# Twelve-layer decoder on one core: where keys, gathered sums, constants and scalings stand in the order of the work

## The chip, the cores and the metric

The kernel runs on one core of a Trainium2 chip, in one launch. The metric is the device time of that core in microseconds (us); the time of a kernel is the median of its runs. TensorE (PE in the profile, PEld for its weight loads), VectorE (DVE), ScalarE (ACT), GpSimd (POOL) and SyncE (SP) each work through their own queue in order, and wait for one another by semaphores.

## The reference

A stack of four decoder layers L0 to L3 on x of shape 8 x 256 x 256 (batches, tokens, features), with a context of 8 x 77 x 256. Each layer has three parts, and every part ends in the same step:

```
x = _layernorm(x + attn(x))
x = _layernorm(x + xattn(x, ctx))
x = _layernorm(x + ffn(x))
```

The parts differ by layer. What matters here:

- L0's and L1's cross-attention have 16 heads of 64 on the context, L1's with a mask. L0's FFN is a mixture of 8 experts, top 2, with GELU; L1's has 8 experts with a capacity and a shared part.
- L1's self-attention is causal softmax attention with 16 heads of 16. L2's self-attention is linear attention with exponential features: keys' features times values are summed first, and the queries' features are multiplied with the sums.
- L2's FFN has 14 routed experts, top 2, and two shared ones that all tokens pass; each is `silu(rms(x) * rw @ W1) @ W2`.
- L3's attention is a state-space block: an RMS norm with weight, an input projection, a short convolution, and decayed sums over chunks of 64 tokens. L3's cross-attention takes the softmax of q within heads and of k over the context, multiplies q with the sums of k and v, and adds q to the result ahead of the output projection.

In an expert layer a token's two results are fetched and added with their weights: `x += w0 * y0 + w1 * y1`, then the norm.

## The kernel before

The 2048 tokens are 16 tiles of 128 tokens (`X[i]`, tokens on the partitions) and four blocks of 512 (`XT`, features on the partitions). `NB` is the eight batches, two tiles each. One class, `Build`, holds the whole kernel; each layer is a method, called in order from `build` (L2705 to 2740). Weights come from a pool `wp` of five buffers of 128 x 2048 (`load_w`, issued on SP). PSUM is a pool of eight banks (`ps`). `mm` at L156 issues the matmuls of most products, `transpose_to` (L294) and `put_xT` (L236) the transposes; their copies out of PSUM alternate between VectorE (L142) and ScalarE (L144). A norm is VectorE's statistics (L250, L252), a power on GpSimd (`rs`, L183 and L184), and VectorE's scaling (L256).

The order of work is written with generators. `later(gen)` puts a generator in a list, `tick` advances the first, `wave` all of them, and `settle` runs them out. A scheduler then orders the instructions on each engine, so neighbours in the source may end apart. `self.mark` names an instruction after which others may be held, with `after`.

**The gathered sums.** `collected` (L2676) gives them batch by batch: for each of two tiles and each of two results an indirect gather on GpSimd (`gy`, L1057), an add on VectorE (L2686), then the norm. `collect(route, behind)` starts it with the first batch. `need(b)` transposes batch b (`put_xT`) and begins the sums of batch b + 1. If `gate` is set, the next add waits for it, and each add becomes the gate of the next one. `gates` holds single ones.

**L0's FFN** (L1136). It computes the keys of L1's cross-attention from the context (`context_keys`, L828: eight slices in two halves of two accumulating matmul pairs each, copied with a bias by ScalarE at L1147), then runs the routed tiles of 256 tokens (`some_tiles`, L1099). For each tile `fetch` gathers an expert's W1, W2 and biases `more` (L1039), and `fetch_x` its tokens (`gx`, L1057); `turned` transposes them; `each(j)` does what goes between tiles. `biased` (L1155, L1157) adds the output biases of the experts after the tiles.

**L1's self-attention** (L1217). Ahead of its loop stand the constants: `mxp` and `vp` set to zeros and ones by GpSimd (L1230, L1233, L1234), masks `later` and `unit` by VectorE. For each batch `project_in` makes k, q, v (L1257, L1262, L1267), `shift` takes the row maxima of the scores (L1287, maxima at L1291) and puts them into the queries (L1300), `weights` the exponentials, `weigh` the result. The loop runs `weights(b)`, then `project_in` and `shift` of b + 1, then `weigh(b)`. `gate` is set to the maxima of batch 0 once, ahead of the loop.

**Routing** (`Routing.batch`). Scores, top 2, the chosen experts' indicators `rsel` (L2541), then a product with a triangular matrix for the ranks. It yields between choice and rank once, for L2 twice.

**L2's self-attention.** Features at L1534 to L1538 (exponential on ScalarE, `min`/`max` on VectorE), projections L1461 and L1467, weighing L1580. `collect` is begun there with one gate, the latest mark (L1488), and no other is set.

**L2's FFN** (L1870). The shared experts' weights `l2s` are scaled by GpSimd (L1882). `l2_shared` makes `xrs` (L1848, L1852), then for two experts the silu products (L1862) and their sums into x (L1868). Block 0 begins ahead of the routing's tables, block 1 in `each(-1)`, after them; blocks 2 and 3 stand in `rest` of `l3_attn`, among the front of L3.

**L3.** `rest` (L1945) mixes the shared experts' steps, two batches of gathered sums at a time (after steps 8 and 16 of a block), and `l3_keys` (L2268 to 2282). `l3_scaled` (L1930) multiplies the weights by the RMS weight on GpSimd. `block` scales four tiles of x by their RMS factor on GpSimd (`xb`, L2005) and transposes them; `steps` makes the decays (`ad`, L2033; `csp`, L2043). The loop over batches takes the next steps of `following` inside `weights` and ahead of `inputs`. In the cross-attention q and the weighted result o are added on GpSimd (L2327), then o is transposed and projected (`project`, L1374).

Of the kernel before, what the change touches and what calls it, by code (L numbers as in the profile page):

```python
# [61 lines left out]
class Build:  # L62
# [765 lines left out]
    def context_keys(self, kT, Wk, copy):  # L828
        hc = NC // 2
        for n in range(8):  # L830
# [201 lines left out]
    def fetch(self, pool, j, table, rows, nf, nb):  # L1032
# [14 lines left out]
        more = get(self.t(pool, [P, nb], "more", bufs=4), "_v")  # L1047
        if 2 * n1 > 2048:
            W1, W2 = (get(self.t(self.wp, [P, 2048], "w"), n) for n in ("_W1t", "_W2t"))
        else:  # L1050
            w = get(self.t(self.wp, [P, 2048], "w"), "_Wt")
            W1, W2 = w[:, :n1], w[:, n1:]
# [46 lines left out]
    def some_tiles(self, px, pool, start, n, route, table, nf, nb, func, scale, bias, each):  # L1099
        nc = self.nc  # L1100
        fetch = lambda j: self.fetch(px, j, table, route.wrow, nf, nb) if j < n else None
        fetch_x = lambda j: self.fetch_x(px, j, route) if j < n else None
        experts, xs = {start: fetch(start)}, {j: fetch_x(j) for j in (start, start + 1)}
# [31 lines left out]
    def l0_ffn(self, route):  # L1135
        nc, a = self.nc, self.a  # L1136
        with ExitStack() as ctx:
# [8 lines left out]
            self.context_keys(  # L1146
                self.l1kT, self.l1wk, lambda o, ps, bias: nc.scalar.activation(o, ps, AF.Identity, bias=bias)  # L1147
            )
# [10 lines left out]
            def each(j):  # L1159
                if j == 1:  # L1160
                    route.places()
                if j == 3:
# [9 lines left out]
            self.routed_tiles(w2, lambda: w2, U0, N0, route, "L0_ffn", 8, 8, AF.Gelu_apprx_tanh, False, True, each)  # L1172
            self.collect(route)
            for i in range(4, NT, 2):
                biased(i)

# [39 lines left out]

    def l1_attn(self):  # L1217
        nc, a = self.nc, self.a
        with ExitStack() as ctx:
# [7 lines left out]

            mxps, vps = [self.t(w1, [P, 4, 4, 32], f"mxp{t}") for t in range(2)], []
            for m in mxps:
                nc.gpsimd.memset(m, 0.0)  # L1230
            for n in range(2):
                v = self.t(w1, [P, 2, H, 32], f"vp{n}")
                nc.gpsimd.memset(v, 0.0)  # L1233
                nc.gpsimd.memset(v[:, :, :, 16:17], 1.0)  # L1234
                vps.append(v)
            rows = [slice(32 * j, 32 * j + 32) for j in range(4)]
            many = lambda m, n: m.unsqueeze(1).to_broadcast([P, n, m.shape[1]])
            later = self.t(w1, [P, 2 * P], "later", BF)
            nc.vector.memset(later[:, :P], 0.0)
            nc.vector.tensor_copy(later[:, P:], self.causb)  # L1240
            unit = self.t(w1, [P, 2 * P], "unit", BF)
# [99 lines left out]
            for b in range(NB):  # L1341
                if b + 1 < NB:
                    self.need(b + 1)
# [127 lines left out]
    def l2_attn(self):  # L1471
        nc, a = self.nc, self.a
        with ExitStack() as ctx:
# [115 lines left out]
            for b in range(NB):  # L1589
                if b + 1 < NB:  # L1590
                    self.need(b + 1)
# [1310 lines left out]
```

## Time and profile before

| what | value |
|---|---|
| three runs | 3620.14, 3611.24, 3616.28 us |
| median | 3616.28 us |
| profiled execution | 3617.24 us |
| its span, first to last instruction | 3615.5 us |
| mean granted clock of TensorE | 0.890 |
| busy VectorE, ScalarE, GpSimd | 50%, 29%, 26% of the span |
| bytes over DMA | 239.49 MB, 66 GB/s |

The stages of the execution, in microseconds from its start: L0's self- and cross-attention to 783, L0's routed tiles 783 to 1083, the turn and L1's self-attention to 1380, L1's cross-attention with its routing to 1716, L1's FFN to 2265, L2's self-attention to 2530, its cross-attention to 2745, L2's FFN to 3010, L3's front to 3165, the loop of its attention to 3376, its cross-attention to 3505, and its FFN to the end.

How to read it: a wait is the idle time of an engine ahead of an instruction, put down to what came last. In a line of waits "PE ps L156 <- DVE w L2282" means that TensorE's instruction of line 156, which writes a tile named ps, waited for VectorE's instruction of line 2282, which writes w. The granted clock is the share of TensorE's full clock that it was allowed. "remote" and "issue" are waits for which the profile shows no releasing engine.

### The profile page before, as it was taken

Reading aid. Unit: us, or ns where it says so; the run is one execution under the profiler, and the core shown is the slowest. Engines: PE = TensorE matmul, PEld = TensorE weight load, DVE = VectorE, ACT = ScalarE, POOL = GpSimd, SP = SyncE. Lnnn points to the kernel's source line nnn. Section 1 sums busy time; section 2 is a strip of 40 time slices with the busy share of each in tenths; the row PEclk is TensorE's granted clock in tenths of the full one; section 3 lists DMA queues with packets and bytes.
Section 4 is the critical chain, followed back from the end, with each engine's and each line's share of the span. In section 5 each row is a group of like instructions: output and inputs, shape, how many; then the busy total and the mean of one; then the engine's idle time right before and its main releaser. Section 6 shows DMA issues by size and latency. Waiting matters only on the chain. (4 is left out here: it accounts for less than half of the span.)

```text
span 3615.5 us, 49376 instructions
## 1 busy us (share of the span) xinstructions
PE 3125.2 (86%) x19135; PEld 2200.5 (61%) x19146; DVE 1825.0 (50%) x4815; ACT 1048.6 (29%) x2351; POOL 926.7 (26%) x1396
## 2 busy tenths in 40 slices
PE   4877589979996998998999999898787997778789
PEld 2443266658884665675555776565565785566556
DVE  7887546531005555776111221575664344677652
ACT  4666322222221333332111111343222111343311
POOL 2222512333314111222000000412334444312251
PEclk7777689979997999988999999999777998888889
DMA  9900100024532000001010333100002452000000
GB/s 336 303 1 1 65 1 18 18 85 175 182 123 90 1 25 13 13 19 57 14 35 0 123 133 113 53 1 7 7 20 97 170 205 75 23 1 7 12 4 21
DMA packets 132128, 239.49 MB, mean 66 GB/s; under 512 B 14568, under 2 KB 103920, under 8 KB 124208
## 3 DMA queue, kind: packets, MB, share of 16 engines
q1 hardware_dynamic: 107632, 136.25, 11.2%
q0 software_dynamic: 23104, 98.95, 7.9%
q8 instruction: 155, 2.54, 0.3%
q10 hardware_dynamic: 1152, 1.05, 0.1%
q14 instruction: 85, 0.70, 0.1%
HBM read 156.52 MB, written 79.69 MB: 65 GB/s over the span
## 5 line engine op out<-in xcount | busy, mean ns | idle before, releaser
L156 PE MATMUL ps<-xt,w 128*128 128x256 f32 (+1 forms) x1408 | 455.7, 474 | 3.3 <-issue 2.9
L156 PE MATMUL ps<-w,hT 128*128 128x256 f32 (+1 forms) x1792 | 397.4, 379 | 0.0
L156 PE MATMUL ps<-gT,w 128*128 128x256 f32 (+1 forms) x1472 | 357.6, 401 | 14.5 <-ACT l1kT L1147 9.6
L156 PEld LDWEIGHTS ps<-w,hT 128*128 128x128 f32 (+1 forms) x1792 | 329.9, 186 | 56.5 <-issue 6.0
L156 PEld LDWEIGHTS ps<-xt,w 128*128 128x128 f32 x1408 | 270.7, 199 | 150.0 <-issue 125.1
L156 PEld LDWEIGHTS ps<-gT,w 128*128 128x128 f32 x1472 | 276.6, 191 | 85.6 <-ACT l1kT L1147 9.8
L156 PE MATMUL ps<-w,oT 128*128 128x256 f32 x768 | 183.2, 392 | 3.3 <-DVE mv L252 1.9
L268 POOL TENSOR_TENSOR xb<-x,rows 128x256 f32<-128x256 f32 x96 | 71.6, 752 | 406.5 <-DVE res L273 398.5
L156 PEld LDWEIGHTS ps<-w,oT 128*128 128x128 f32 x768 | 147.3, 196 | 38.9 <-issue 15.3
L236 PE MATMUL ps<-ident,x 128*128 128x128 f32 x320 | 63.8, 314 | 78.3 <-DVE x L256 57.7
L1117 ACT ACTIVATE hT<-ps,more 128x256 f32<-128x256 f32 x152 | 71.9, 474 | 196.3 <-PE ps L156 189.5
L256 DVE TENSOR_SCALAR x<-res,mv,rs 128x256 f32<-128x256 f32 x128 | 57.4, 449 | 126.0 <-POOL rs L184 126.0
L1128 DVE COPY y<-ps 128x512 f32<-128x512 f32 x41 | 28.3, 690 | 174.7 <-PE ps L156 156.4
L1191 DVE TENSOR_TENSOR hT<-hT,ps 128x512 f32<-128x512 f32 x56 | 38.5, 687 | 154.3 <-PE ps L156 152.9
L934 PE MATMUL ps<-ident,P 128*77 128x128 f32 x512 | 90.7, 305 | 29.7 <-POOL P L925 20.8
L678 ACT ACTIVATE e<-ps,nm 128x128 bf16<-128x128 f32 (+1 forms) x256 | 103.9, 458 | 40.0 <-DVE nm L673 24.0
L1672 POOL TENSOR_TENSOR kpad<-kpad,rows 128x256 f32<-128x256 f32 (+1 forms) x10 | 7.3, 730 | 404.3 <-DVE hu L1621 317.0
L184 POOL TENSOR_TENSOR rs<-rs,mhalf 128x1 f32<-128x1 f32 x192 | 105.9, 553 | 14.2
L934 PEld LDWEIGHTS ps<-ident,P 128*77 128x77 f32 x512 | 61.3, 158 | 78.5 <-issue 26.4
L925 POOL TENSOR_TENSOR P<-P,z 128x1232 f32<-128x1232 f32 x24 | 54.0, 2251 | 211.4 <-DVE z L923 205.1
L949 PE MATMUL ps<-PT,V 77*64 77x256 f32 x512 | 99.8, 451 | 6.4 <-DVE PT L142 5.1
L1187 ACT ACTIVATE hT<-ps 128x512 f32<-128x512 f32 x56 | 33.4, 597 | 237.6 <-PE ps L156 237.6
(656 smaller groups left out, 6336.2 us busy)
## 6 DMA issues: line engine op xcount, KB each, us to landing
l2x<-zero SPq DMA_DIRECT2D x28, 1024.0 KB
l0x<-zero SPq DMA_DIRECT2D x16, 1024.0 KB
w<-in_L_ffn_rg SPq DMA_DIRECT2D x8, 1024.0 KB
w<-in_L_ffn_ru SPq DMA_DIRECT2D x8, 1024.0 KB
w<-in_L_ffn_rd SPq DMA_DIRECT2D x8, 1024.0 KB
l2e<-y SPq DMA_DIRECT2D x22, 256.0 KB
rows<-in_rows SPq DMA_DIRECT2D x9, 544.0 KB
l0e<-y SPq DMA_DIRECT2D x19, 256.0 KB
```

Source lines behind the costliest of these rows:

```text
L156: self.nc.tensor.matmul(out, lhsT, rhs, start=(i == 0), stop=(i == last))
L184: self.nc.gpsimd.tensor_tensor(out, out, self.mhalf[: in_.shape[0], :w], ALU.pow)
L236: self.nc.tensor.transpose(ps[:, k * P : (k + 1) * P], x[:, k * P : (k + 1) * P], self.ident)
L256: nc.vector.tensor_scalar(t, r, mv[:, 0:1], rs, ALU.subtract, ALU.mult)
L268: self.nc.gpsimd.tensor_tensor(t, self.X[i], row, ALU.add)
L678: nc.scalar.activation(e[:, : (t + 1) * P], ps[j][:, i, :], AF.Exp, bias=nm[:, t, h : h + 1], accum_out=z[:, t, h : h + 1],)
L925: eng.tensor_tensor(pr, pr, z.unsqueeze(2).to_broadcast([P, H, SC]), ALU.mult)
L934: nc.tensor.transpose(psv[:, m, t * P : (t + 1) * P], Pt[t][:, 2 * n + m, :], self.ident)
L949: nc.tensor.matmul(po[64 * m : 64 * m + 64, :S], V[:, h * 64 : (h + 1) * 64], ahead[n % 2][:, m, :], start=True, stop=True,)
L1117: nc.scalar.activation(hT[:, f + m, :], ps[:, m * 256 : (m + 1) * 256], func, bias=more[:, f + m : f + m + 1])
L1187: nc.scalar.activation(hT[:, f, :], ps, func, **({"bias": bias(f)} if bias else {}))
L1191: nc.vector.tensor_tensor(hT[:, f, :], hT[:, f, :], ps, ALU.mult)
```

## The change

1. L1's context keys are made in two parts: three of eight slices ahead of L0's tiles, five after them and after `biased`, with a second load of the 1 MB of Wk on SP.
2. For the first tile of a routed layer the tokens are gathered between the weights W1 (or W) and what follows; `more` is gathered after W1.
3. L1's constants are made by `l1_constants`, called at tile 2 of L0, in a pool of its own that lives until the end of L1's self-attention.
4. In the self-attention of L1 and L2 the gate is set anew in every batch, ahead of `need(b + 1)`: to the latest maxima in L1, to the latest features in L2. 
5. L3's cross-attention: `project` has an argument `plus`; the transposed o and the transposed q are added by VectorE as it takes o out of PSUM. ScalarE copies all the transposed q (three buffers each). GpSimd's add is gone.
6. The scalings of `l2s`, of L3's weights and of x in `block` are ScalarE's activations instead of GpSimd's.
7. In L2's FFN the first step of the second shared block (`xrs`) stands ahead of the start of the tiles.
8. In `rest` one batch of sums is due per four steps or so of the shared experts instead of two or more at steps 8 and 16; the first two steps of `block(0)` are filled with 9 and 7 steps instead of 6 and 6.
9. In L3's loop the remaining steps of `following` come after `settle(1)`, and none inside `weights`.
10. `Routing.batch` yields twice between choice and rank in L1 too.

The diff, cut to its core:

```diff
-    def context_keys(self, kT, Wk, copy):
+    def context_keys(self, kT, Wk, copy, ns=range(8)):
...
-        for n in range(8):
+        for n in ns:
...
-        more = get(self.t(pool, [P, nb], "more", bufs=4), "_v")
+        more = self.t(pool, [P, nb], "more", bufs=4)
         if 2 * n1 > 2048:
-            W1, W2 = (get(self.t(self.wp, [P, 2048], "w"), n) for n in ("_W1t", "_W2t"))
+            W1 = get(self.t(self.wp, [P, 2048], "w"), "_W1t")
+            if between is not None:
+                between()
+            get(more, "_v")
+            W2 = get(self.t(self.wp, [P, 2048], "w"), "_W2t")
...
-        experts, xs = {start: fetch(start)}, {j: fetch_x(j) for j in (start, start + 1)}
+        xs = {}
+        experts = {start: fetch(start, lambda: xs.update({start: fetch_x(start)}))}
+        xs[start + 1] = fetch_x(start + 1)
...
+            self.context_keys(self.l1kT, self.l1wk, with_bias, range(3))
...
+                if j == 2:
+                    self.l1_constants()
...
+            Wk = self.load_w(a["L1_xattn_Wk"], 2, 1024)
             self.collect(route)
             for i in range(4, NT, 2):
                 biased(i)
+            self.context_keys(self.l1kT, Wk, with_bias, range(3, 8))
...
+    def l1_constants(self):
+        nc, pool = self.nc, self.l1s_pool
+
+        mxps, vps = [self.t(pool, [P, 4, 4, 32], f"mxp{t}") for t in range(2)], []
+        for m in mxps:
+            nc.gpsimd.memset(m, 0.0)
+        for n in range(2):
+            v = self.t(pool, [P, 2, H, 32], f"vp{n}")
+            nc.gpsimd.memset(v, 0.0)
+            nc.gpsimd.memset(v[:, :, :, 16:17], 1.0)
+            vps.append(v)
...
+        self.l1c = mxps, vps, later, unit
...
             q2 = shift(0, q, k)
-            self.gate = self.mark
             for b in range(NB):
                 if b + 1 < NB:
+                    self.gate = self.mark
                     self.need(b + 1)
...
-    def project(self, b, both, W, row, pool, route=None, late=False):
+    def project(self, b, both, W, row, pool, route=None, late=False, plus=None):
...
+                ps = self.ps()
+                for k in range(2):
+                    self.nc.tensor.transpose(ps[:, k * P : (k + 1) * P], o[:, k * P : (k + 1) * P], self.ident)
+                self.nc.vector.tensor_tensor(oT, ps[:, :D].rearrange("p (k n) -> p k n", k=2), plus[t], ALU.add)
...
-                    nc.vector.scalar_tensor_tensor(f[:, j], ps[j], 1.0, f[:, j], ALU.max, ALU.min)
+                    self.mark = nc.vector.scalar_tensor_tensor(f[:, j], ps[j], 1.0, f[:, j], ALU.max, ALU.min)
...
             for b in range(NB):
                 if b + 1 < NB:
+                    self.gate = self.mark
                     self.need(b + 1)
                 kvT = sums(kp, v)
...
-                nc.scalar.activation(hT[:, f, :], ps, AF.Silu)
+                self.mark = nc.scalar.activation(hT[:, f, :], ps, AF.Silu)
...
-                nc.gpsimd.tensor_scalar(v, v, self.fm("l2f_rw")[:, c : c + 1], 1.0, ALU.mult, ALU.mult)
+                nc.scalar.activation(v, v, AF.Copy, scale=self.fm("l2f_rw")[:, c : c + 1])
...
             route.tables(N2)
+            second = self.l2_shared(w4, 1, route.r)
+            next(second)
...
-                self.nc.gpsimd.tensor_scalar(w[:, k, :], w[:, k, :], self.fm(name)[:, k : k + 1], 1.0, ALU.mult, ALU.mult)
+                self.nc.scalar.activation(w[:, k, :], w[:, k, :], AF.Copy, scale=self.fm(name)[:, k : k + 1])
...
+                due = {(2, 8): 0, (2, 12): 1, (2, 16): 2, (3, 4): 3, (3, 8): 4, (3, 14): 5, (3, 16): 6}
...
-                        if k in (8, 16):
+                        if (blk, k) in due:
                             self.gates.append(self.mark)
-                            self.need({(2, 8): 1, (2, 16): 3, (3, 8): 4, (3, 16): 6}[blk, k])
+                            self.need(due[blk, k])
...
-                    nc.gpsimd.tensor_scalar(x, self.X[4 * blk + t], r[:, t : t + 1], 1.0, ALU.mult, ALU.mult)
+                    nc.scalar.activation(x, self.X[4 * blk + t], AF.Copy, scale=r[:, t : t + 1])
...
-            for _ in range(2):
-                next(front)
-                fill(6)
+            next(front)
+            fill(9)
+            next(front)
+            fill(7)
...
-                if b % 2:
-                    next(following, None)
                 return E, xd
...
                 if b + 1 < NB:
-                    if b % 2:
-                        for _ in following:
-                            pass
                     cv, zs = inputs(b + 1, xrs[(b + 1) // 2])
                     next(following, None)
                 self.settle(1)
+                if b % 2:
+                    for _ in following:
+                        pass
...
-                    qT = self.t(w2, [P, 2, P], f"qT{t}")
-                    self.transpose_to(qT, q[:, t, :], 2)
+                    qT = self.t(w2, [P, 2, P], f"qT{t}", bufs=3)
...
+                    nc.scalar.copy(qT, ps[:, :D].rearrange("p (k n) -> p k n", k=2))
...
-                    nc.gpsimd.tensor_tensor(o, o, q[:, t, :], ALU.add)
...
-        if kind == 2:
+        if kind:
             yield
```

## The prediction

> **What bounds the kernel now.** I read the page's first two parts, then TensorE's waits, then the busy table by stretches, and last the stretches one by one in the timeline.
>
> ```profile
> PE 3125.2 (86%) x19135; PEld 2200.5 (61%) x19146; DVE 1825.0 (50%) x4815; ACT 1048.6 (29%) x2351; POOL 926.7 (26%) x1396
> ...
> PEclk7777689979997999988999999999777998888889
> ```
>
> TensorE is busy for 3125.2 of 3615.5 us; nothing else comes near. So the kernel is bound by TensorE, and what is left is its idle time, 490 us, and matmuls run at less than full clock: the last row falls to 7 and 8 tenths at the turns between layers. In TensorE's waits the reader is to see which of them this change can reach:
>
> ```profile
> PE ps L236 <- DVE x L256: 57.7, 28, 10.5
> ...
> PE ps L156 <- DVE rsel L2541: 28.4, 17, 3.1
> ...
> PE ps L156 <- DVE w L2282: 17.0, 3, 14.6
> PE ps L294 <- POOL o L2327: 13.8, 11, 2.3
> PE ps L156 <- issue: 13.8, 3, 9.6
> PE ps L156 <- DVE ad L2033: 12.1, 3, 5.8
> PE ps L294 <- POOL xb L2005: 12.1, 4, 5.6
> PE ps L1284 <- DVE x L2686: 11.5, 1, 11.5
> ```
>
> The columns are total, times, longest. Then the table by stretch (span, then busy time of PE, PEld, DVE, ACT, POOL, the granted clock, DMA share, GB/s): L0's tiles, the turn to L1 attention, L1's routing, the L2 turn and loop, the L2 FFN front, the L3 front, loop and cross-attention:
>
> ```profile
> 783.00:1083.00 300.00, 290.15 (x1361) 247.21 (x1359) 29.68 (x46) 79.10 (x165) 89.04 (x95) 0.98 0.47 166
> 1083.00:1166.00 83.00, 52.25 (x336) 35.40 (x340) 46.53 (x102) 11.48 (x23) 42.45 (x57) 0.73 0.30 99
> 1380.00:1716.00 336.00, 303.12 (x1731) 217.07 (x1732) 226.82 (x650) 106.73 (x233) 79.43 (x105) 0.86 0.08 26
> 2265.00:2310.00 45.00, 31.48 (x112) 17.83 (x112) 24.35 (x58) 11.44 (x17) 30.78 (x42) 0.81 0.23 68
> 2310.00:2530.00 220.00, 195.01 (x1833) 129.82 (x1843) 143.51 (x330) 95.64 (x171) 41.22 (x92) 0.96 0.03 11
> 2745.00:2815.00 70.00, 50.92 (x177) 32.94 (x170) 27.93 (x113) 8.88 (x18) 29.39 (x35) 0.75 0.43 150
> 3010.00:3165.00 155.00, 113.16 (x445) 76.51 (x444) 87.10 (x252) 38.54 (x58) 73.47 (x121) 0.85 0.16 52
> 3165.00:3376.00 211.00, 168.93 (x1000) 138.88 (x999) 162.05 (x415) 89.93 (x144) 44.38 (x75) 0.86 0.01 3
> 3376.00:3505.00 129.00, 94.29 (x418) 71.39 (x419) 73.63 (x208) 24.22 (x46) 64.80 (x104) 0.83 0.03 9
> ```
>
> The first row is a stage that TensorE fills; every edit outside a row with idle TensorE is worth nothing. The edits all lie in or just before rows with 20 to 42 us idle.
>
> **What the Trainium skill says.** "TensorE: Matmul & The Clock Gate", section "What's actually happening": the clock is halved after an idle window of about 3.4 us and full again after about 3.4 us of work. The trace agrees on the first: after the gaps of 4 us and more the granted clock is 0.50 (3179.5 to 3200, 13.9 us of matmuls); coming back takes 3.4 to 20 us here. So a closed gap is also worth the slow work behind it. "GPSIMD Engine Reference", "Key points": GpSimd shares its SBUF interfaces with VectorE. At 1099.6 the L256 scaling takes 2.38 us beside a memset of vp, 0.45 on average. "ScalarE: Activation LUTs", "What ACT_TABLE_LOAD costs": a switch of tables 1283 ns, which the trace shows exactly; a 256-column activation with a pointer operand works out (an estimate from that page) at 280 + 0.833 x 256 = 0.49 us, and the trace has 0.474 (L1117).
>
> **The change, part by part.** I compared the order of the instructions on each engine in both programs: all moves described do happen there.
>
> A, keys in two parts, x gathered before `more` and W2. Before, 64 key matmuls take 18.94 us (775.6 to 794.6), then TensorE idles 9.60 us behind the copies L1147; the first tile starts at 804.6. 40 of the 64 go behind the tiles: 40 x 18.94/64 = 11.8 us less in front. But ScalarE, VectorE and TensorE's own semaphores all stood still until 797 to 803.5 ("remote" in the timeline), and I can't tell what holds them while 5 MB of gathers land. If that stall is by the clock on the wall, 1 us is gained; if not, up to 15. I take 9. The six memsets now ahead of the last scatters on GpSimd (2 x 0.52 + 2 x 0.94 + 2 x 0.16 = 3.2 us) lie in its idle stretches of 2.7 to 6.2 us; up to 2 without that cover, inside the bounds.
>
> B, turn to L1. The 40 matmuls return here: 11.8 us into two gaps of 10.52 and 3.37, so they are hidden. The new 1 MB load goes first in SP's queue, and Wqk, Wq and Wv stand behind it; at the 390 GB/s of that stretch it is 2.7 us (estimate), while Wqk is not wanted for 10 us. Gone with the constants: 2.38 - 0.45 = 1.9 us; and 32 projections at half clock took 9.0 us, 7 at full: 2. Gain 4 (bounds: a late Wk costs 1; all of it gains 7).
>
> C, sums held in L1's loop. VectorE works through up to 16 L2686 adds, each waiting for its gather (1.25 us apart on GpSimd), ahead of project_in's L1257. TensorE idles 11.54 + 1.86 us, and from 1143.0 to 1165.6 does 8.4 us of work at clock 0.55, about 5 at full. Held to four a block, behind L1300, they lie in blocks of 34 us with VectorE busy 17. 22.6 - 5 = 17.6 is the most; I take 16 (12 to 18).
>
> D, one more yield before the rank. Waits for rsel are 12.5 us in 8 in L1's cross-attention; another slice of matmuls covers most. 7 (4 to 9).
>
> E, the same hold in L2. Turn gaps of 2.69, 2.87, 4.86 and 3.11 us and half clock for 10 us speak for 11; but a block of 26 us has TensorE busy 25 and VectorE 17.5, and gets four adds (0.48), two L250 (0.39), two L252 (0.15), two L256 (0.41): 3.9 us, and two waits for rs of 0.9, 5.7 us in VectorE's queue. They come behind the copies of project_in's products, while TensorE has projections and weighing of its own. Gain 6 (from 11 to a loss of 8).
>
> F, FFN front of L2. l2s scaling leaves GpSimd (1.36 us ahead of rs; a gap of 3.93 there), and xrs L1852 comes before the tables. The gap of 9.58 us ahead of 2809.2 stands as "issue", with VectorE's xrs late in the same "remote" manner as in A; 2.6 us of slow work follow. Gain 8 (0 to 12: it is 0 if that stall isn't xrs's).
>
> G, L3 front, 3010 to 3165. 41.8 us of idle: L2282 17.0, xb 10.8, kv L2252 10.6. GpSimd has L1930's 6.5 us, four gathers of 1.25 and the rs chain in one queue; mv of 3035.65 gets its rs at 3041.9. Scaling goes to ScalarE, 5.8 us by the page's price, busy only 38.5 of 155 there; three to four groups of hTs matmuls go ahead of xb's transposes; sums come one per four steps. Two more table loads in all, 2.6 us. I take half of the idle time, 20 (8 to 30; the low end is ScalarE waiting for weights that land at 3025 with silus queued behind).
>
> H, L3 loop. `following` moved: two waits for ad of 5.77 and 5.45 us, then half clock over 25.4 us of matmuls (13.9 + 11.5). Half of the 11.2, since L2177 and zs (8.2 and 6.4 us) are next, and half of 25.4/2: 5.6 + 6.3, say 11 (3 to 16).
>
> I, o + q. 13.8 us of TensorE's waits are for L2327 (16 x 0.73 us). The add now rides on the copy of the transpose at VectorE (0.42 instead of a shared copy: eight more, 3.4 us, with 73.6 of 129 busy), qT all on ScalarE. The next to come last is L256 (13.8 us in 6). Half: 7 (0 to 10).
>
> Sum: 9 + 4 + 16 + 7 + 6 + 8 + 20 + 11 + 7 = 88. The profiled execution took 3617.24 (span 3615.5 and 1.7 around it); 3617.24 - 88 = 3529.2. The median of the runs is 1.0 below that execution: 3528. With all low ends the sum is 20, with all high ends 128; as they are independent I take 3503 to 3553 as this case's own range.
>
> **The rivals.** First, stalls that merely move: A and F are stalls by the wall clock, and in G to I the next wait takes over. For it: "remote" names no engine, and L256 is last for 57.7 us, mostly untouched. Then C, D and a third of the rest: 16 + 7 + 65/3 = 45, so 3571. Second, more than I count: each closed gap also brings its clock back, near all high ends: 3491. Against it: every stage would have to close. Third, slower: in the loops of L1 and L2 a held add waits for its gather at the head of VectorE's queue, and everything behind it, the copies and features that free PSUM, waits too. It decides from the point where VectorE's 17.5 + 5.7 us and the landing no longer fit the 26 us of a block (slack 3 us). Then each of 10 blocks pays 5 for the wait and 5 for the halved clock; that is 100 against the 88, and the time is 3629. Against it: the gathers have a whole block for themselves, and the adds stand where VectorE has little to do. Last, the loops absorb all and nothing changes (3617); that the moves don't take place is excluded by the order of the instructions.
>
> **Chances.** Forecast 0.64, moved stalls 0.19, more 0.10, no change 0.03, slower 0.04. The range reaches down to 3490 and up to 3580, which leaves out the last two and the fringes. About 0.3%, 11 us, is what a measurement of this kernel can tell from no change: faster 0.93, same 0.03, slower 0.04.
>
> **What would show it.** A: the first tile's matmuls at about 795 instead of 804.6; at 803 it was the wall clock. B: no gap over 3 us between 1091 and 1106 of before. C: no wait for L2686. D: rsel under 6 us in L1. E: the four turn gaps gone and blocks still 26 us; 30 would be the third rival. F: no 9.6 us of "issue". G: the wait for L2282 under 5 and none for xb. H: none over 3 for ad. I: none for L2327, with L256 not above 20. The mean clock should rise from 0.89 to about 0.92. I am wrong if TensorE's waits keep their sum under other names.

## The result, and the profile after

The kernel before takes 3615.9 us, the changed one 3582.0 (3578.9 to 3584.2): ratio 0.9906, interval 0.9889 to 0.9923. A second measurement on another chip gave 0.9884 (0.9869 to 0.9899). The change gains 34 to 42 us; 88 were forecast, and 3582.0 lies above the stated range, which reached up to 3580.

The page after, busy times and the granted clock in slices:

```profile
PE 3118.9 (87%) x19135; PEld 2191.0 (61%) x19146; DVE 1821.6 (51%) x4815; ACT 1062.9 (30%) x2383; POOL 901.2 (25%) x1350
...
PEclk7777689979999998998999999999777999888899
```

TensorE is busy for 3118.9 us, against 3125.2 before, and idle for 463.6 of its span, against 490.3. So idle time has shrunk by 27 us, not by most of 88: the sign that I had set for being wrong (the waits keep their sum under other names) is largely there. The mean clock has only come up from 0.890 to 0.900; the forecast wanted 0.92. Slice 13, the turn to L1, rose from 7 tenths to 9. TensorE's waits after (total, times, longest):

```profile
PE ps L236 <- DVE x L256: 45.7, 26, 5.1
...
PE ps L934 <- DVE P L925: 21.9, 8, 4.4
...
PE ps L156 <- DVE rsel L2569: 17.4, 10, 2.8
...
PE ps L1551 <- DVE f L1561: 15.4, 15, 4.9
PE ps L156 <- DVE w L2308: 13.6, 5, 6.5
...
PE ps L294 <- DVE csp L2070: 11.9, 3, 4.5
PE ps L156 <- DVE oT L1402: 11.0, 8, 3.5
PE ps L156 <- issue: 10.5, 3, 4.9
...
PE ps L294 <- ACT xb L2032: 9.8, 4, 3.5
```

The waits that the change aimed at are gone or smaller: L2686, ad and L2327 are not in the list, rsel has 17.4 instead of 28.4, L256 45.7 instead of 57.7. In their place stand waits that were small or not there before: the features L1561 (1.6 before), csp L2070 (1.4), oT L1402 (0.3), and P L925 on VectorE (the probabilities of the softmax in the cross-attention, 8.8). The stretches after, in the order of before (turn to L1, the rest of L1's self-attention, L1's routing, L2's turn, L2's loop, L3's front, its loop):

```profile
1072.00:1147.00 75.00, 66.84 (x448) 47.03 (x452) 38.20 (x81) 16.56 (x33) 22.90 (x32) 0.89 0.28 95
1147.00:1366.00 219.00, 201.21 (x1961) 139.57 (x1952) 123.79 (x278) 65.28 (x137) 46.99 (x84) 0.99 0.08 23
1366.00:1686.00 320.00, 285.17 (x1728) 200.25 (x1728) 222.73 (x625) 105.17 (x232) 76.50 (x104) 0.91 0.08 27
2235.00:2268.00 33.00, 27.44 (x111) 16.43 (x110) 13.93 (x30) 10.76 (x17) 11.36 (x17) 0.90 0.10 29
2268.00:2506.00 238.00, 199.92 (x1832) 131.87 (x1842) 154.53 (x358) 96.07 (x171) 60.74 (x116) 0.94 0.06 19
2986.00:3132.00 146.00, 115.76 (x443) 76.06 (x442) 82.67 (x251) 46.55 (x77) 61.45 (x102) 0.88 0.17 55
3132.00:3345.00 213.00, 172.37 (x1001) 140.83 (x1000) 161.59 (x413) 96.04 (x153) 40.31 (x68) 0.88 0.01 3
```

L2's loop is the row to look at: it took 220 us with 195.0 of TensorE busy and takes 238 with 199.9. So TensorE's idle time there rose from 25 to 38 us, and its matmuls took 5 us longer at a clock of 0.94 instead of 0.96. VectorE and GpSimd are busier by 11 and 20 us, with the sums that stood at the turn before.

For the account by stage I took the same instructions in both traces and the median shift of their start at the end of each stage. The second pair is both kernels profiled on one chip of the experiments (before_again, after_again).

| stage (time in the trace before) | forecast | first pair | second pair |
|---|---|---|---|
| to 760, unchanged | 0 | -2.9 | -2.9 |
| A, L0's start and tiles, to 1083 | -9 | -7.3 | -10.4 |
| B, turn, to 1125 | -4 | +3.8 | +5.5 |
| C, L1's first sums, to 1166 | -16 | -17.9 | -17.8 |
| C, the rest of the loop, to 1381 | in it | +10.3 | +7.9 |
| D, L1's routing, to 1716 | -7 | -16.2 | -12.7 |
| E, L2's turn, to 2310 | -6 | -11.5 | -11.4 |
| E, L2's loop, to 2530 | in it | +18.2 | +18.3 |
| F, L2's FFN front, to 2820 | -8 | -6.5 | -4.6 |
| L2's tiles, to 3005 | 0 | +6.3 | +1.7 |
| G, L3's front, to 3165 | -20 | -8.6 | -9.9 |
| H, L3's loop, to 3376 | -11 | +2.0 | +6.1 |
| I, L3's cross-attention, to 3505 | -7 | -2.5 | -2.8 |

A minus is a gain. The three stages between that are not listed move by less than 1. In L2's tiles of the first pair, TensorE waited 3.0 us at 2935 while ScalarE, VectorE and GpSimd stood at "remote" waits; the second pair has no such stall. A stage's figure depends on where it is cut, by some 2 us, and the first row shows that a stage without any edit moves by 2.9.

### The profile page after: what moved, and what is told of

Read it like the earlier page. It is cut to its first block, busy times and chain, and to the rows that moved or that the text cites. A ratio compares the mean times of both kernels' runs of the same rounds, so it can differ in the third digit from the quotient of the medians.

```text
span 3582.5 us, 49358 instructions
## 1 busy us (share of the span) xinstructions
PE 3118.9 (87%) x19135; PEld 2191.0 (61%) x19146; DVE 1821.6 (51%) x4815; ACT 1062.9 (30%) x2383; POOL 901.2 (25%) x1350
## 3 DMA queue, kind: packets, MB, share of 16 engines
q1 hardware_dynamic: 107904, 137.30, 11.5%
## 5 line engine op out<-in xcount | busy, mean ns | idle before, releaser
L156 PEld LDWEIGHTS ps<-w,oT 128*128 128x128 f32 x768 | 148.4, 197 | 49.2 <-issue 12.7
L934 PE MATMUL ps<-ident,P 128*77 128x128 f32 x512 | 94.7, 313 | 42.7 <-DVE P L925 21.9
L256 DVE TENSOR_SCALAR x<-res,mv,rs 128x256 f32<-128x256 f32 x128 | 56.2, 439 | 128.6 <-POOL rs L184 128.5
L236 PE MATMUL ps<-ident,x 128*128 128x128 f32 x320 | 61.9, 308 | 64.7 <-DVE x L256 45.7
L184 POOL TENSOR_TENSOR rs<-rs,mhalf 128x1 f32<-128x1 f32 x192 | 106.3, 554 | 14.8
L925 POOL TENSOR_TENSOR P<-P,z 128x1232 f32<-128x1232 f32 x24 | 54.0, 2251 | 209.9 <-DVE z L923 203.6
L1560 ACT ACTIVATE f<-ps,neg 128x512 f32<-128x512 f32 x128 | 77.3, 689 | 76.5 <-PE ps L1557 72.1
```

What stands on the lines that cost most here:

```text
L156: self.nc.tensor.matmul(out, lhsT, rhs, start=(i == 0), stop=(i == last))
L184: self.nc.gpsimd.tensor_tensor(out, out, self.mhalf[: in_.shape[0], :w], ALU.pow)
L236: self.nc.tensor.transpose(ps[:, k * P : (k + 1) * P], x[:, k * P : (k + 1) * P], self.ident)
L256: nc.vector.tensor_scalar(t, r, mv[:, 0:1], rs, ALU.subtract, ALU.mult)
L925: eng.tensor_tensor(pr, pr, z.unsqueeze(2).to_broadcast([P, H, SC]), ALU.mult)
L934: nc.tensor.transpose(psv[:, m, t * P : (t + 1) * P], Pt[t][:, 2 * n + m, :], self.ident)
```

## The experiments

Each kernel is the changed kernel with one edit or with two of them together, and is timed against the kernel before on its own chip; its stages are set against the trace of before from the second pair. rs_first, l2_unheld, l1_unheld and keys_whole ran on a chip that is 1% faster as a whole (3581 us for the kernel before, which was not profiled there). So of them only ratios, and stages among themselves, are compared; if the ratios above hold there, which was not measured, the changed kernel takes 3539 to 3547 (an estimate). L2's turn and loop come out within 1 us of each other in every kernel whose edit leaves them alone, on all chips. L1's routing and L3's front differ by up to 4 us between such kernels on one chip (by 8 in l1_unheld), and L1's routing by 10 between chips.

**Why the loops lost.** In L2's loop of the changed kernel, GpSimd (start, duration, line, what it does):

```profile
2358.68 1.14 POOL L1064 DMA_INDIRECT gy<-l1e,rsrc  x1 [16.15 <-DVE x L2714]
2360.12 0.98 POOL L1064 DMA_INDIRECT gy<-l1e,rsrc  x1 [0.30 <-DVE mv L252]
2361.41 0.95 POOL L1064 DMA_INDIRECT gy<-l1e,rsrc  x1 [0.31 <-issue]
2362.42 0.19 POOL L183 TENSOR_SCALAR rs<-mv 128x1 f32<-128x1 f32 x1
2362.88 0.97 POOL L1064 DMA_INDIRECT gy<-l1e,rsrc  x1 [0.27 <-issue]
2363.88 0.58 POOL L184 TENSOR_TENSOR rs<-rs,mhalf 128x1 f32<-128x1 f32 x1
```

VectorE meanwhile (a wait and what ended it stand in brackets):

```profile
2360.78 0.18 DVE L252 BATCH_NORM_AGGREGATE mv<-st 128x2 f32<-128x6 f32 x1
2364.49 0.41 DVE L256 TENSOR_SCALAR x<-x,mv,rs 128x256 f32<-128x256 f32 x1 [3.53 <-issue]
2365.40 0.41 DVE L256 TENSOR_SCALAR x<-x,mv,rs 128x256 f32<-128x256 f32 x1 [0.50 <-POOL rs L184]
2365.73 2.47 DVE L1561 SCALAR_TENSOR_TENSOR f<-ps,f 128x512 f32<-128x512 f32 x4
```

and TensorE:

```profile
2366.46 0.38 PE L1551 MATMUL ps<-ones,onesb 128*128 128x512 bf16 x1 [3.53 <-DVE f L1561]
```

The statistics of both tiles are ready by 2360.96, but the first rs only at 2364.46. In GpSimd's order of instructions, which is the same in both traces of the changed kernel, the gathers of the next batch stand ahead of this rs and between its two steps (L183 and L184). The first starts as an add frees its buffer, and the four take 1.3 to 1.5 us each from start to start. VectorE's queue stands 3.53 us at L256, the features L1561 are behind it, and TensorE's next feature product, which needs the PSUM that L1561 reads, waits 3.53 us too. Four blocks of the loop have such a wait at L256, of 3.0 to 4.4 us. Four runs on this:

```diff
 rs_first
...
-                    g.gather(y, self.eo, self.src[:, k, i : i + 1])
+                    got = g.gather(y, self.eo, self.src[:, k, i : i + 1])
+                    if b:
+                        g.after(got.ins, [roots[2 * b - 1].ins])
```

> The changed kernel (3582 us), with the gathers of a batch's results held on GpSimd until the two rs of the batch before have been made. My theory: the held sums cost time in the loops because the next batch's four gathers (1.25 us each) get ahead of their rs on GpSimd, so VectorE stands 3.5 us at L256 in each of L2's blocks and 1.8 in L1's, with the features behind it. Then L2's loop gives back 12 to 17 us, L1's 5 to 9 and the turn to L1 3: 3555 to 3562, and TensorE's wait for the features (15.4 us) falls under 4. The rival: the 3.8 us of VectorE work per block itself is the cost. Then the wait stays at 12 to 15 and the time is within 4 us of 3582.

Measured: 3527.8 us, ratio 0.9853 (0.9838 to 0.9868); 11 to 19 us less than the changed kernel's ratios give, where 20 to 27 were expected. The wait for L1561 fell from 15.4 to 7.6 us. L2's loop lost 11.4 us instead of 18.3, L1's 3.4 instead of 7.7, L3's front gained 17.2 instead of 10; the turn to L1 stayed. So the gathers were in the way, but over half of L2's loss remained: they now stood ahead of the block's own norm (L256 of that norm waited 3.1 us in two blocks and 5.5 in a third).

```diff
 l2_unheld
                 if b + 1 < NB:
-                    self.gate = self.mark
                     self.need(b + 1)
                 kvT = sums(kp, v)
```

> The changed kernel with the hold of the sums in L2's self-attention taken back (the gate is not set anew). By the account of the two traces the hold gains 11 us at the turn and loses 17.5 in the loop: taking it back gives 6 us, 3576. If the loop's loss is from something else (the later start of the loop, the clock), the turn's 11 us come back as a loss: 3593.

Measured: 3540.0 us, ratio 0.9890 (0.9875 to 0.9905). L2's turn and loop together stand at 0.0 against the kernel before; with the hold they lose 6.7. The stages answer as expected; the whole time lies inside the estimate for the changed kernel and can't show 6 us.

```diff
 l1_unheld
+            self.gate = self.mark
             for b in range(NB):
                 if b + 1 < NB:
-                    self.gate = self.mark
                     self.need(b + 1)
```

> The changed kernel with the hold of the sums in L1's self-attention taken back to one gate ahead of the loop. By the account of the two traces the hold gains 18 us by 1165 and loses 9 until 1300: taking it back costs 9, 3591. If the loss in the blocks is not the hold's, it costs the whole 18: 3600.

Measured: 3553.6 us, ratio 0.9926 (0.9912 to 0.9939), 7 to 15 us slower than the changed kernel. L1's self-attention is as before (+0.6 instead of -10.2): both the gain of 18 and the loss of 8 are the hold's. L1's routing was 8 us shorter than in its three neighbours, though its edit does not touch that stage; it had 14 us at half clock after 1620 where l2_unheld had 34.

The next takes away both collisions: in each loop the gathers are issued after the block's own norm.

```diff
 late_gathers
+        def fetched(b):
+            if b < NB and b not in got:
...
+                        ins = g.gather(y, self.eo, self.src[:, k, i : i + 1]).ins
+                        if b:
+                            g.after(ins, [g.root.ins])
...
                 self.settle()
+                self.fetch_sums(b + 3)
```

> The changed kernel with the gathers of each later batch held behind the latest rs, and in L1's and L2's self-attention issued only after the block's own norm. In the run before this with only the first of the two, L2's loop still lost 11 us against the kernel before, because the four gathers (5 us on GpSimd) now stood ahead of xb and rs of the block's own norm. My theory: with GpSimd's queue free for both norms, L2's loop loses 2 to 6 us, L1's 0 to 3, and the ratio falls from 0.985 to 0.983. The rival: VectorE's 3.8 us of added work per block is what remains: L2's loop keeps losing 9 to 12 and the ratio stays at 0.985.

Measured: 3554.9 us, ratio 0.9828 (0.9815 to 0.9842). L2's loop loses 5.9 instead of 18.3, L1's 3.8. GpSimd in a block of that kernel, the last rs of the block's norm and then the gathers, with nothing behind them:

```profile
2354.28 0.55 POOL L184 TENSOR_TENSOR rs<-rs,mhalf 128x1 f32<-128x1 f32 x1
2355.11 1.07 POOL L1064 DMA_INDIRECT gy<-l1e,rsrc  x1 [0.28 <-POOL rs L184]
2356.48 0.95 POOL L1064 DMA_INDIRECT gy<-l1e,rsrc  x1 [0.30 <-issue]
2357.74 0.94 POOL L1064 DMA_INDIRECT gy<-l1e,rsrc  x1 [0.30 <-issue]
2358.99 0.95 POOL L1064 DMA_INDIRECT gy<-l1e,rsrc  x1 [0.30 <-issue]
```

and VectorE's waits for rs in it, the two of the sums and the first of the block:

```profile
2346.43 0.41 DVE L256 TENSOR_SCALAR x<-x,mv,rs 128x256 f32<-128x256 f32 x1 [0.73 <-POOL rs L184]
...
2348.35 0.41 DVE L256 TENSOR_SCALAR x<-x,mv,rs 128x256 f32<-128x256 f32 x1 [0.95 <-POOL rs L184]
...
2353.95 0.41 DVE L256 TENSOR_SCALAR x<-res,mv,rs 128x256 f32<-128x256 f32 x1 [1.26 <-POOL rs L184]
```

They are 0.7 to 1.3 us, about what I had put down for the hold (0.9). What remains, 6 us in L2, may be VectorE's own added work; that was not tried apart.

**The turn to L1 and the keys.**

```diff
 keys_whole
-            self.context_keys(self.l1kT, self.l1wk, with_bias, range(3))
+            self.context_keys(self.l1kT, self.l1wk, with_bias)
...
-            Wk = self.load_w(a["L1_xattn_Wk"], 2, 1024)
...
-            self.context_keys(self.l1kT, Wk, with_bias, range(3, 8))
```

> The changed kernel with all of the context keys ahead of L0's tiles again (the second part and its load of 1 MB left out); constants and the order of the gathers stay changed. By the account of the two traces the first tiles start 8 us later and the turn to L1 gets 5 us shorter: 3585. If the turn's new gap of 4.9 us is VectorE's queue (x of batch 1 waiting for rs ahead of the copy of xt), it stays without the keys too and grows, and the time is 3590 or more.

Measured: 3546.0 us, ratio 0.9905 (0.9889 to 0.9920). Against its three neighbours on that chip, L0's start is 4.7 us later and the turn 8.7 shorter. So splitting the keys gave 4.7 of the 13.2 us of A on that chip and cost more at the turn; the other 8.5 come with the other edits there, which were not taken back one by one. At the turn VectorE and TensorE of the changed kernel:

```profile
1098.90 0.41 DVE L256 TENSOR_SCALAR x<-x,mv,rs 128x256 f32<-128x256 f32 x1 [3.53 <-POOL rs L184]
1100.53 0.41 DVE L142 COPY xt<-ps 128x256 f32<-128x256 f32 x1
```

```profile
1082.42 13.27 PE L156 MATMUL ps<-cT,w 128*128 128x308 f32 x40
...
1101.04 8.83 PE L156 MATMUL ps<-xt,w 128*128 128x256 f32 x32 [4.91 <-issue]
```

and TensorE of keys_whole:

```profile
1086.43 9.90 PE L156 MATMUL ps<-xt,w 128*128 128x256 f32 x32 [0.68 <-ACT xt L144]
```

The 40 key matmuls run until 1095.7, though x of batch 0 is ready for its transposes at 1091.4. Without them TensorE waits 6.61 and 2.13 us for x: so 13.27 us of keys fill 8.74 us of gaps and reach 4.5 beyond. The transposes come later by this. In VectorE's order of instructions the copy of xt then stands behind the sums and the norm of batch 1, and not ahead of them, and the wait before the projections is 4.91 us instead of 0.68. Together these are the 8.7 us. The expectation that such a wait would stay without the keys was wrong.

```diff
 xt0_act
-                    g.put_xT(i, g.X[i])
+                    g.put_xT(i, g.X[i], None if b else nc.scalar.copy)
```

> The changed kernel with both copies of batch 0's transposed x after a layer's sums on ScalarE instead of one on each engine. My theory: at the turn to L1 TensorE's gap of 4.9 us (5 to 8 us, called issue) is this copy, standing on VectorE behind the L256 of batch 1, which waits for rs behind gathers. Then the gap goes and the turn is 4 to 6 us shorter; nothing else moves by over 2. The rival: TensorE waits there for a weight (Wqk behind the new 1 MB load): the turn stays within 1 us.

Measured: 3578.2 us, ratio 0.9893 (0.9878 to 0.9908). TensorE's projections of the turn:

```profile
1094.02 6.31 PE L156 MATMUL ps<-xt,w 128*128 128x256 f32 x28 [0.71 <-ACT xt L237]
```

0.71 us instead of 4.91: the turn is 7 to 9 us shorter, so it was the copy in VectorE's queue, not a weight. But L1's loop lost 14.8 instead of 8 to 11, which the expectation did not have, and the whole time hardly moved.

**Both together.** The edits of late_gathers and xt0_act.

> The changed kernel with the gathers behind the norms (as in late_gathers, ratio 0.983) and batch 0's xt copies on ScalarE (as in xt0_act, turn to L1 7 us shorter). If the two add: ratio 0.980 to 0.981. If the copies only let the sums of batch 1 collide later (L1's loop lost 4 us in that run): 0.982 to 0.983.

Measured: 3533.4 us, ratio 0.9782 (0.9767 to 0.9798): 79 us under the kernel before, more than the two add up to and more than expected. The turn gains some 2 us, L1's loop after its first sums loses 3.3, L2's turn gains 17 to 19 and its loop loses 4.8; L3's front gains some 14. Where the surplus over the sum comes from was not traced, nor was it tried what these two edits would give the kernel before.

**L1's routing.**

```diff
 one_yield
-        if kind:
+        if kind == 2:
             yield
```

> The changed kernel with one yield between choice and rank in L1's routing again. By the account of the two traces that edit gains 15 us, twice what I had put down, because the waits for rsel had each also cost clock: 15 us slower than the changed kernel here. If half of it came from elsewhere in that stage, 7.

Measured: 3589.2 us against 3572.5 for the changed kernel on the same chip, ratios 0.9936 (0.9923 to 0.9950) and 0.9884. The stage is 13.7 us longer (+1.0 instead of -12.7). So the gain is this edit's.

**L3.** The reference runs of the second pair:

> The kernel before, run and profiled on the chip of the experiments, so that each stage can be compared on one chip: the ratio is 1, and the profile shows which stages are shorter here than in the first profile.

> The changed kernel on the chip of the experiments. If the ratio of the first measurement (0.9906) holds here too, and the kernel before takes 3581 us here, it takes 3547 us, and the stages give and take as in the first two profiles: L1's routing 15 less, L2's loop 17 more, L3's front 8 less, L3's loop and cross-attention within 3.

Measured: 3609.2 and 3572.5 us, ratios 0.9992 (0.9983 to 1.0000) and 0.9884. The stages repeat within 4 us or so, those of L3's loop within 4.1; only L2's tiles, with the stall at 2935, differ by 4.6.

```diff
 following_back
+                if b % 2:
+                    next(following, None)
                 return E, xd
...
+                    if b % 2:
+                        for _ in following:
+                            pass
                     cv, zs = inputs(b + 1, xrs[(b + 1) // 2])
...
-                if b % 2:
-                    for _ in following:
-                        pass
```

> The changed kernel with the steps of `following` in L3's loop at their old places. My theory: moving them only put csp's waits (11.9 us in 3) in the place of ad's (12.1 in 3), so L3's loop is within 3 us of the changed kernel's. The rival: the move did gain, and ScalarE's xb (9.8 us of waits) and its table loads took it away; then taking it back costs 6 to 12 us.

Measured: 3569.8 us, ratio 0.9877 (0.9862 to 0.9892); L3's loop +7.3 against +6.1. The move gained nothing: with it ad's waits (12.1 us) are gone and csp's come (11.9), without it csp has 1.4 and ad 5.8. What took ad's place is seen on VectorE in the changed kernel, whose queue is full with the convolution's products ahead of csp:

```profile
3166.96 1.66 DVE L2127 SCALAR_TENSOR_TENSOR w<-xpad,fmt,w 128x256 f32<-128x256 f32 x4
...
3168.86 0.87 DVE L2127 SCALAR_TENSOR_TENSOR w<-xpad,fmt,w 128x256 f32<-128x256 f32 x2
...
3170.17 0.28 DVE L2070 TENSOR_SCALAR csp<-ps 128x128 f32<-128x128 f32 x1
```

```profile
3170.51 1.12 PE L294 MATMUL ps<-ident,csp 128*128 128x128 f32 x4 [4.46 <-DVE csp L2070]
```

```diff
 xb_back
-                    nc.scalar.activation(x, self.X[4 * blk + t], AF.Copy, scale=r[:, t : t + 1])
+                    nc.gpsimd.tensor_scalar(x, self.X[4 * blk + t], r[:, t : t + 1], 1.0, ALU.mult, ALU.mult)
```

> The changed kernel with x scaled on GpSimd again in L3's block (xb), the other scalings on ScalarE. My theory: in L3's loop ScalarE's exponentials and table loads delay xb (waits of 3.2 and 3.5 us), which GpSimd had ready in time before; moving it back gains 4 to 8 us in the loop and costs 2 to 5 in L3's front. The rival: the waits move to csp and ad, and the loop stays within 2 us.

Measured: 3579.0 us, ratio 0.9890 (0.9875 to 0.9905); loop +3.2 and front -11.3 against +4.7 to +6.1 and -9.9 to -10.7 for the changed kernel. My theory was wrong: no cost in the front, and a gain in the loop of 1.5 to 3 us, below what the stage repeats to; csp's waits stayed (5.0, 3.8, 3.6 us).

l3_loop_back is following_back and xb_back together.

> The changed kernel with both edits of L3's loop taken back (following at its old places, xb on GpSimd). My theory: each edit alone is covered by the other's wait, and together they cost the loop the 2 to 6 us that it lost; without them the loop is as before, 2 to 6 shorter. The rival: the loop's time is VectorE's (76% busy, its queue full around csp) whatever the order, and stays within 2 us of the changed kernel's.

Measured: 3573.4 us, ratio 0.9884 (0.9866 to 0.9901). In the loop nothing is left of a shift until 3340 (0.0), and 3 us are lost at its end; the changed kernel stood at 5.3 by 3340. Over the whole loop that is a loss of 3.1 us instead of 4.7 to 6.1, and xb_back alone has 3.2. These differences are no larger than what the stage repeats to, and the whole time is the changed kernel's: that the two edits cost the loop, or hide each other, is not shown.

```diff
 l3_order_back
-                due = {(2, 8): 0, (2, 12): 1, (2, 16): 2, (3, 4): 3, (3, 8): 4, (3, 14): 5, (3, 16): 6}
+                due = {(2, 8): 1, (2, 16): 3, (3, 8): 4, (3, 16): 6}
...
-            fill(9)
-            next(front)
-            fill(7)
+            for _ in range(2):
+                next(front)
+                fill(6)
```

> The changed kernel with the sums of L3's front due two or more at a time again, and block 0 filled with 6 and 6 steps (edit 8 taken back), the scalings still on ScalarE. My theory: this order is what moved silu work ahead of the waits for L2282 (17.0 to 13.6 us) and xb; without it the front is 4 to 9 us longer. The rival: the scaling did all of it, and the front stays within 2.

Measured: 3584.4 us, ratio 0.9919 (0.9904 to 0.9935); the front gains 1.5 instead of 9.9.

```diff
 l3_scale_back
-                self.nc.scalar.activation(w[:, k, :], w[:, k, :], AF.Copy, scale=self.fm(name)[:, k : k + 1])
+                self.nc.gpsimd.tensor_scalar(w[:, k, :], w[:, k, :], self.fm(name)[:, k : k + 1], 1.0, ALU.mult, ALU.mult)
```

> The changed kernel with L3's weights scaled on GpSimd again (6.5 us in its queue ahead of rs), xb still on ScalarE. My theory: rs comes late again and the front is 3 to 8 us longer. The rival: the same rs waits behind gathers anyway, and ScalarE is freed for the silus (a wait of 4.4 us for hTs), so the front is the same within 2 or shorter.

Measured: 3578.6 us, ratio 0.9910 (0.9896 to 0.9925); the front gains 7.0 instead of 9.9. The order of the work did most of the gain (8.4 us). The scaling's 3 are not above what the front differs by between kernels that leave it alone.

```diff
 oq_back
-                yield from self.project(b, both, W[:, :, 768:1024], "l3x_bp", w2, late=True, plus=qTs)
+                yield from self.project(b, both, W[:, :, 768:1024], "l3x_bp", w2, late=True)
...
+                    nc.gpsimd.tensor_tensor(o, o, q[:, t, :], ALU.add)
```

The copies of the transposed q are as before again too.

> The changed kernel with o and q added on GpSimd again in L3's cross-attention. By the account of the two traces the edit gained 2.5 to 3 us of the 7 that I had put down, because oT on VectorE (11.0 us of waits in 8) took the place of o on GpSimd (13.8 in 11): 3 us slower in this stage, all others alike. If it gained nothing, within 1.

Measured: 3586.0 us, ratio 0.9916 (0.9902 to 0.9929); the stage is 3.9 us longer (+1.2 instead of -2.7).

The edits of F, and the separate edits of A ahead of L0's tiles, were not taken back.

## Why the prediction was wrong

The bound was read rightly, and the sign. The sum was wrong: 88 against 34 to 42. In both pairs of traces 55 us are missing. C and E, the hold of the sums, make 19 to 21 of them, H 13 to 17, G 10 to 11, B 8 to 10 and I 4 to 5; D gave 6 to 9 more than forecast.

- **The step that failed first is the hold of the sums, in E and C**: "two waits for rs of 0.9, 5.7 us in VectorE's queue". I priced the sums in their new place with the waits of norms that had GpSimd to themselves, and looked at VectorE's room only. I had counted the gathers in L3's front as a thing in rs's way, but not here, where they stand right between the statistics and the power: in the block shown one wait of 3.53 us and one of 0.50. L2's loop lost 18.3 us where I had reckoned a few, L1's 8 to 10. rs_first and late_gathers show this: with the gathers behind the norms the two loops lose 5.9 and 3.8. C's first 17.9 and E's 11.4 at the turn came as forecast or better. This is the third rival in its kind and place (a wait at the head of VectorE's queue with features behind it), and its sign showed: blocks of L2 with held sums took 27 to 31 us, not 26. But its reason was wrong, rs and not the gather's landing, and its price was 26 to 29 us over both loops, not 100.
- **H** was to gain 11 and lost 2 to 6; this is the second step that failed. The waits for ad went, but TensorE's idle time in the loop hardly did (42.1 us before, 40.6 after), because csp came last instead, where I had named L2177 and zs. And the other half of the forecast, 6 us of clock, rested on a wrong order of events. In the trace of before, the granted clock was at half before the first of the long waits began:

```profile
3179.50:3185.10 5.60, 5.26 (x24) 4.88 (x24) 3.34 (x12) 3.66 (x4) 1.13 (x3) 0.50 0.00 0
```

```profile
3190.89 1.00 PE L156 MATMUL ps<-ad,triu 128*128 128x8 f32 x4 [5.77 <-DVE ad L2033]
```

  The wait began at 3185.1, the half clock at 3179.5. So closing that wait could not be counted on to bring the clock back, and the time at half clock in the loop was 58 and 52 us before in the two pairs, 51 and 59 after. Why the loop lost 2 to 6 us stays open.
- **B** was to gain 4 and lost 4 to 6. The gaps of 10.52 and 3.37 us in the trace of before are 6.61 and 2.13 in keys_whole, with the other edits in place and on another chip, so the keys reached beyond them; and I had not looked at the queue behind: the copy of xt stood on VectorE behind batch 1's L256, again at an rs behind gathers. keys_whole and xt0_act show it.
- **G** was mis-sized: 9 to 10, not 20. Half the idle time was a guess without a view behind it: the waits for L2282 and xb were to fall under 5 and to nothing, and have 13.6 and 9.8 us. Most of the gain is the order's. What is left is partly the same collision: with the gathers behind the norms the front gains 14 to 17. The two more table loads came as counted (54 instead of 52, 1283 ns each). 1283 ns is the load alone: the Trainium skill, "ScalarE: Activation LUTs", section "What ACT_TABLE_LOAD costs", puts a whole switch, with draining, at about 2.66 us, but in the traces here a load can begin 18 ns after the activation ahead of it.
- **I**: 2.5 to 4, not 7; oT's 11.0 us of waits on VectorE took the place of o's 13.8, where I had named L256.
- **D** gave 13 to 16, not 7, and not for my reason. The waits for rsel fell from 12.5 to 1.8 us, but those for P L925 on VectorE rose from 8.8 to 21.9. By the rows above TensorE was idle for 32.9 us of the stage before and 34.8 after. What fell is its busy time, from 303.1 to 285.2, with the clock at 0.91 instead of 0.86. In the second pair the time at half clock fell from 103 to 65 us, and one_yield has 92. In before_again, TensorE around one of the waits for rsel (span, busy PE, PEld, DVE, ACT, POOL, clock):

```profile
1454.00:1457.40 3.40, 2.59 (x16) 1.59 (x16) 2.72 (x18) 1.65 (x4) 0.00 (x0) 1.00 0.00 0
1457.40:1460.80 3.40, 2.86 (x18) 1.44 (x20) 2.02 (x12) 0.47 (x1) 0.00 (x0) 1.00 0.00 0
1460.80:1471.00 10.20, 10.20 (x74) 8.90 (x72) 7.84 (x23) 4.64 (x10) 4.42 (x4) 0.50 0.16 55
```

  A wait of 1.16 us at 1456.6 is followed by 10.2 us at half clock. So the edit gained, as one_yield shows, but through the clock and not through shorter waits; why the waits for P cost less clock than those for rsel is not shown.
- **A** came out at 7 to 10 for 9, in part by luck: 9 was a value between two readings, and the split keys, on which it was reckoned, were worth 4.7. The first tile's matmuls start at 788.7 instead of 804.6 (2.9 us of this come from before the stage), so the stall there did not keep its place on the wall clock. **F** was near (4.6 to 6.5 for 8), and its wait of 9.6 us is gone.

The chance of 0.19 for stalls that merely move was too small: its time, 3571, is nearer than mine, and its mechanism (the next wait takes over) is what D, H and I did.

## What to carry to other kernels

When work is moved between others, follow each of its waits to the queue that answers it, and ask what else stands in that queue ahead of the answer: here the gathers that a freed buffer let go stood between a norm's statistics and its power, and four of them together blocked VectorE for 3.0 to 4.4 us, and TensorE behind it for 3.5 to 4.9 in three blocks. A hold on a consumer needs a hold on its producer too; with both, and one copy moved out of the blocked queue, the changed kernel stands 79 us under the one before instead of 34 to 42. A closed gap only counts when the next instruction in each queue involved has been looked at.

## What the hardware showed beyond that

- The granted clock fell to half after two stretches in which TensorE was busy 2.59 and 2.86 of 3.40 us (the rows at 1454 above). The Trainium skill, "TensorE: Matmul & The Clock Gate", section "What's actually happening", speaks of an idle window of about 3.4 us; no such window stands here. But the same matmuls in the first trace of before kept the full clock for another 20 us:

```profile
1455.60:1459.00 3.40, 2.70 (x18) 1.70 (x16) 2.60 (x18) 1.65 (x4) 0.00 (x0) 1.00 0.00 0
1459.00:1462.40 3.40, 2.74 (x18) 1.32 (x20) 2.02 (x12) 0.47 (x1) 0.00 (x0) 1.00 0.00 0
```

  Both pairs of stretches are busy for 5.4 of 6.8 us, and only one was followed by half clock. So a wait of 1 us among small products can be followed by 10 us at half clock, and these traces don't show what decides it.
- One indirect gather of 128 rows keeps GpSimd's queue for 1.25 us (0.95 and 0.30 up to the next), whether its data is wanted soon or not.
- The kernel before took 3581 us on one chip and 3609 to 3617 on the others. The changed kernel's ratio was taken on two of the others and agrees within 0.3% (0.9906 and 0.9884).
